# First mixture of experts of a four-layer decoder: the shared expert ahead of the routing, TensorE in written order, biases joined

## The chip, the cores and the metric

The kernel runs on one core of a Trainium2 chip, in one launch. The metric is device time in microseconds, from the program's start to its end; the time given is the median of three runs. One more execution was recorded by the hardware profiler, instruction by instruction; all durations come from that one. A core has five engines with an instruction queue each, which run in parallel and wait for each other on semaphores: TensorE (PE, with its weight loads shown as PEld), VectorE (DVE), ScalarE (ACT), GpSimd (POOL) and SyncE (SP, which here only issues DMAs).

## What is computed

The whole kernel is a decoder of four layers on x of 16 sequences x 128 tokens x 256 features in float32. Each layer adds a self-attention, a cross-attention and a feed-forward block to x, each behind a layer norm. The change concerns only the feed-forward block of layer 0, a mixture of 32 routed experts and one shared expert. Cut to this block, with x the 2048 normalized tokens:

```python
logits = x @ Wr + br                                   # 256 -> 32
aff = sigmoid(logits)
top_v, top_i = top_k(aff, 8)
top_w = top_v / (sum(top_v) + 1e-9)
w_full = zeros(T, 32); w_full[token, top_i] = top_w    # 8 of 32 are not zero
shared = (silu(x @ Wg_s + bg_s) * (x @ Wu_s + bu_s)) @ Wd_s + bd_s
gate = silu(einsum('th,ehi->eti', x, Wg) + bg)         # 256 -> 128 for each expert
up = einsum('th,ehi->eti', x, Wu) + bu
down = einsum('eti,eih->eth', gate * up, Wd) + bd      # 128 -> 256
return shared + einsum('te,eth->th', w_full, down)
```

Every expert is computed for every token; the weight w_full is zero where a token doesn't use it. The bias of the second product, bd, is weighted with w_full too, so that all 32 of them are one product: w_full @ bd.

## The kernel before

x stays in SBUF in four tiles `x[g]` (`NG` = 4 groups of `GB` = 4 sequences, so `GT` = 512 tokens a group, tokens on the 128 partitions). Tiles come from pools. `b1` is a pool of four PSUM banks of 512 float32 columns, `b2` one of two tiles of 1024 columns (two banks each). A tile asked for while all buffers of its tag are in use waits until an old one has been read out. Expert weights share seven SBUF slots (`slot`, 3 x 256 columns each) with other weights.

A scheduler orders the instructions of each engine: it may take an instruction ahead of an earlier one when it counts it ready sooner. Only what goes through `keep_in_program_order` (helpers `pinned` and `pinned_transpose`, L253 to L258) stays in the written order among itself. Before the change the feed-forward block uses `self.mm` (L162 to L168), which isn't pinned; the attention blocks ahead of it use pinned products.

`l0_ffn` (L563) has three parts.

1. For each group (L590 to L616): `layernorm` (statistics on VectorE at L201 and L202, square root on ScalarE and reciprocal on VectorE at L191 and L192, then normalization by VectorE's `tensor_scalar` at L205 into `h`); `hidden_T` (eight transposes by TensorE at L183 into two banks, which `evac` copies in turn by VectorE at L110 and ScalarE at L112 into `hT`); the router product of 8 matmuls with 32 columns; bias, sigmoid, and a chain of small VectorE instructions (the eight largest, sum, reciprocal, L603 to L611) which leaves the weights in `w_all`.
2. For each group (L618 to L628): four transposes of `w_all` at L622 into `wT`, a copy out, and for each sequence a bias product of two matmuls: `wT` with `bd` (32 rows, L166) and a row of ones with `bd_s` (1 row, L168). VectorE adds each result to x (L220).
3. For the shared expert (e = -1) and then the 32 experts, for each group, one unit (L629 to L649): `gate` and `up`, two matmuls of 512 columns each; SiLU with bias on ScalarE (L638) and a multiplication on VectorE (L639) into `gs`; `down`, four matmuls of 256 columns into a `b2` tile; and on VectorE the addition to x (L644 for the shared expert, L649 with the token's weight otherwise). 33 x 4 = 132 units.

A float32 matmul shows in the profile as two records: 132 x 2 matmuls of `gate` are 528 records. A transpose is one record.

Ahead of this block stands the cross-attention of layer 0. Its last work for group 3 is three additions by GpSimd (L548 to L550), which complete `x[3]`. Behind it stands the self-attention of layer 1; its preparation (`c2b`, `c2col` products on TensorE, centers and scales on VectorE) doesn't depend on x, and the scheduler places it inside the last experts. All DMAs of the block are issued by SP; those of the router weights, of `bd` and `bd_s` and of the first experts stand near the start of the program.

Of the kernel before, what the change touches and what calls it, by code (L numbers as in the profile page):

```python
# [8 lines left out]
F = mybir.dt.float32  # L9
BF = mybir.dt.bfloat16  # L10
U32 = mybir.dt.uint32
AF = mybir.ActivationFunctionType
ALU = mybir.AluOpType
# [3 lines left out]
P = 128  # L17
B = 16
T = B * P
DM = 256  # L20
DC = 192
NG = 4
GB = B // NG
GT = GB * P
# [5 lines left out]
class Decoder:  # L30
# [532 lines left out]
    def l0_ffn(self):  # L563
        nc = self.nc
        E, K = 32, 8
        wr = self.wp.tile([P, 2, E], F, tag="wr", name="wr")
        self.load_into(wr, "L0_ffn_Wr")
        bd = self.wp.tile([E, DM], F, tag="bd", name="bd")
        nc.sync.dma_start(out=bd, in_=self.a["L0_ffn_bd"])
        bds = self.row("L0_ffn_bd_s")  # L570

        def expert(e):
            w = self.slot([P, 3, DM], "expert")
# [7 lines left out]
            return w  # L581

        with self.tc.tile_pool(name="l0f", bufs=1) as wk:
            hTs = []

            w_all = wk.tile([P, B * E + P], F, tag="w_all", name="w_all")
            nc.gpsimd.memset(w_all[:, B * E :], 0.0)
            for g in range(NG):
                hT = self.hidden_T(self.layernorm(g))
                hTs.append(hT)  # L590
                ps = self.b1("router")[:, 0 : GB * E]
                for t in range(GB):
                    self.mm(ps[:, t * E : (t + 1) * E], [(hT[:, k, t * P : (t + 1) * P], wr[:, k, :]) for k in range(2)])
                aff = wk.tile([P, GB, E], F, tag="aff", name="aff", bufs=2)
                nc.vector.tensor_tensor(
                    aff, ps.rearrange("p (t e) -> p t e", e=E), self.b("L0_br").unsqueeze(1).to_broadcast([P, GB, E]), ALU.add
# [18 lines left out]
                    ALU.mult,  # L615
                )  # L616

            for g in range(NG):  # L618
                ps = self.b1("wT")
                for t in range(GB):  # L620
                    o = (g * GB + t) * E
                    nc.tensor.transpose(ps[:, t * P : (t + 1) * P], w_all[:, o : o + P], self.ident)  # L622
                wT = wk.tile([E, GT], F, tag="wT", name="wT", bufs=2)
                self.evac(wT, ps[0:E, :])
                for t in range(GB):
                    po = self.b1("bd")[:, 0:DM]
                    self.mm(po, [(wT[:, t * P : (t + 1) * P], bd)], bds)
                    self.add_x(g, t, po)  # L628
            for e in range(-1, E):  # L629
                w = expert(e)  # L630
                bg = self.c("L0_bg_s") if e < 0 else self.c("L0_bg")[:, e : e + 1]
                bu = self.c("L0_bu_s") if e < 0 else self.c("L0_bu")[:, e : e + 1]
                for g in range(NG):
                    pg, pu = self.b1("gate"), self.b1("up")
                    for i, ps in ((0, pg), (1, pu)):
                        self.mm(ps, [(w[:, i, k * P : (k + 1) * P], hTs[g][:, k, :]) for k in range(2)])
                    gs = wk.tile([P, GT], F, tag="gs", name="gs", bufs=3)
                    nc.scalar.activation(gs, pg, AF.Silu, bias=bg)  # L638
                    nc.vector.scalar_tensor_tensor(gs, pu, bu, gs, ALU.add, ALU.mult)  # L639
                    pd = self.b2("down").rearrange("p (t d) -> p t d", t=GB)  # L640
                    for t in range(GB):
                        self.mm(pd[:, t, :], [(gs[:, t * P : (t + 1) * P], w[:, 2, :])])
                    if e < 0:
                        nc.vector.tensor_tensor(self.x[g], self.x[g], pd, ALU.add)  # L644
                        continue
                    for t in range(GB):
                        o = (g * GB + t) * E + e
                        xt = self.x[g][:, t, :]
                        nc.vector.scalar_tensor_tensor(xt, pd[:, t, :], w_all[:, o : o + 1], xt, ALU.mult, ALU.add)  # L649

# [1571 lines left out]
```

## Time and profile before

| | before |
|---|---|
| median of three runs | 3755.2 us (3746.98 to 3758.4) |
| profiled execution | 3759.38 us, span 3757.7 us |
| TensorE (matmul) busy | 3406.1 us, 91% of the span |
| VectorE busy | 2112.9 us, 56% |
| ScalarE busy | 1414.6 us, 38% |
| GpSimd busy | 534.0 us, 14% |
| mean granted TensorE clock | 0.936 |
| first `gate`, start of last expert `down` in the trace | 436.8 us, 1123.2 us |

Times in the trace count from the span's start. A line of groups names the source line, the engine, the operation, the tiles written and read, the count, the busy time, the mean of one, and the idle time of the engine just before with what ended it. The chain that ended last is followed back from the last instruction, at each step to what released it. The list of waits gives for pairs of instructions how long the first one's engine sat idle until the second one ended. The clock column is the share of full TensorE clock that was granted. A busy TensorE isn't TensorE at full speed: at half clock it is as busy and takes twice as long.

### The profile page before, as it was taken

The page shows a single profiled execution, that of the slowest core. Times are in us where ns is not written, and L with a number is a line of the kernel's source. Part 1 is how long each engine was busy: PE and PEld are TensorE (multiplying, and loading weights), DVE is VectorE, ACT ScalarE, POOL GpSimd, SP SyncE. Part 2 cuts the span into 40 slices and gives each one's busy share as a digit, 9 for nine tenths or more (in the row PEclk, how much of TensorE's full clock was granted, in tenths as well). Part 3 has the DMA queues.
Part 4 walks back from the last instruction along what each step waited for, and adds up shares of the span by engine and source line. Part 5 has one row for each costly group of instructions (what it writes and reads, how often), then busy time and mean ns, then how long its engine had stood idle before and what let it go on. Part 6 is the DMA issues. An engine that isn't in the chain of part 4 may idle for free.

```text
span 3757.7 us, 51557 instructions
## 1 busy us (share of the span) xinstructions
PE 3406.1 (91%) x21008; PEld 1839.0 (49%) x21008; DVE 2112.9 (56%) x4132; ACT 1414.6 (38%) x1923; POOL 534.0 (14%) x686
## 2 busy tenths in 40 slices
PE   7987999999998899986799999467899999999999
PEld 4555655555556556663355566344222222224665
DVE  5545344444464444455577744514699999983440
ACT  2344111111124422226556523012477677774221
POOL 5423000000002321115100021012200000002100
PEclk9988699999998999998899999588799999999989
DMA  3000000000010100010000000083502020000000
GB/s 95 8 2 5 5 17 21 17 21 20 27 48 6 37 1 1 1 41 6 13 1 1 12 3 1 33 298 101 111 22 30 11 31 11 11 1 25 1 8 17
DMA packets 90485, 105.47 MB, mean 28 GB/s; under 512 B 11364, under 2 KB 72678, under 8 KB 89990
## 3 DMA queue, kind: packets, MB, share of 16 engines
q1 hardware_dynamic: 79672, 89.71, 9.0%
q0 software_dynamic: 4224, 6.43, 0.5%
q10 hardware_dynamic: 6352, 6.03, 0.5%
q8 instruction: 165, 2.70, 0.3%
q14 instruction: 72, 0.59, 0.1%
HBM read 85.53 MB, written 16.60 MB: 27 GB/s over the span
## 4 chain that ended last, share of the span: by engine, by line
PE 79%; DVE 9%; ACT 4%; POOL 3%; issue 3%; DMA 1%; POOLq 0%; ACTq 0%; DVEq 0%
PE acc L1784 7%; PE down L166 6%; PE gate L166 6%; PE up L166 6%; PE st L1784 6%; PE proj L255 6%; PE one L1784 4%; PE st L255 4%; PE qT L166 3%; PE o L255 2%; PE h L255 2%; PE rb L255 2%; PE v L886 2%; PE fc L166 2%; PE pr L166 2%
## 5 line engine op out<-in xcount | busy, mean ns | idle before, releaser
L1916 DVE TENSOR_REDUCE mx<-one 128x1 f32<-128x512 f32 x1024 | 660.1, 686 | 50.8 <-PE one L1784 40.5
L2039 ACT ACTIVATE e<-st 128x1024 f32<-128x1024 f32 x512 | 496.8, 1021 | 208.0 <-PE st L1784 206.9
L649 DVE SCALAR_TENSOR_TENSOR x<-down,w_all,x 128x256 f32<-128x256 f32 x512 | 212.2, 477 | 315.1 <-PE down L166 315.1
L638 ACT ACTIVATE gs<-gate,cols 128x512 f32<-128x512 f32 x132 | 90.7, 687 | 584.3 <-PE gate L166 584.3
L1784 PE MATMUL acc<-e,v 128*32 128x512 f32 x2048 | 288.9, 616 | 1.7 <-ACT e L2039 1.7
L1784 PE MATMUL st<-qp,kp 113*128 113x512 bf16 x1024 | 274.0, 388 | 9.8 <-ACT e L2039 5.7
L166 PE MATMUL gate<-hT,expert 128*128 128x512 f32 x528 | 250.0, 596 | 0.0
L166 PE MATMUL down<-expert,gs 128*128 128x256 f32 x1056 | 249.4, 379 | 0.5 <-DVE gs L639 0.5
L166 PE MATMUL up<-hT,expert 128*128 128x512 f32 x528 | 249.3, 594 | 0.0
L166 PEld LDWEIGHTS down<-expert,gs 128*128 128x128 f32 x1056 | 200.6, 190 | 84.0 <-DVE gs L639 31.7
L1784 PE MATMUL one<-kp,qp 16*128 16x512 bf16 x1024 | 224.1, 394 | 13.3 <-DVE mx L1916 7.3
L1784 PEld LDWEIGHTS <-qp 16*128 16x128 bf16 x1024 | 49.5, 91 | 332.1 <-issue 328.7
L166 PEld LDWEIGHTS gate<-hT,expert 128*128 128x128 f32 x528 | 100.7, 191 | 126.8 <-issue 126.5
L1784 PEld LDWEIGHTS <-kp 113*128 113x128 bf16 x1024 | 79.2, 98 | 148.8 <-issue 86.8
L988 DVE TENSOR_TENSOR cT<-o,rb 128x512 f32<-128x512 f32 x64 | 44.3, 691 | 164.2 <-ACT rb L986 164.2
L166 PEld LDWEIGHTS up<-hT,expert 128*128 128x128 f32 x528 | 100.9, 191 | 72.3 <-issue 65.7
L986 ACT COPY rb<-rb 128x512 f32<-128x512 f32 x64 | 37.5, 585 | 252.5 <-PE rb L255 252.5
L166 PE MATMUL qT<-hT,L_xattn_Wq 128*128 128x512 f32 x256 | 116.8, 610 | 8.6 <-DVE hT L110 4.5
L1187 DVE SCALAR_TENSOR_TENSOR xs<-xBC,cols,xs 128x508 f32<-128x508 f32 x144 | 106.1, 741 | 22.2 <-ACT xs L1183 18.8
L718 POOL MEMSET v<- 128x256 f32 x16 | 5.2, 329 | 794.6 <-DVE x L649 750.6
L255 PE MATMUL o<-e,v 128*32 128x128 f32 (+1 forms) x2048 | 105.8, 280 | 11.8 <-DVE nm L292 11.8
L639 DVE SCALAR_TENSOR_TENSOR gs<-up,cols,gs 128x512 f32<-128x512 f32 x132 | 99.0, 751 | 24.9 <-PE up L166 8.7
(511 smaller groups left out, 5697.7 us busy)
## 6 DMA issues: line engine op xcount, KB each, us to landing
W<-in_L_ffn_W_dram SPq DMA_DIRECT2D x46, 512.0 KB, 4.5
expert<-in_L_ffn_Wg_dram SPq DMA_DIRECT2D x32, 128.0 KB, 2.2
expert<-in_L_ffn_Wu_dram SPq DMA_DIRECT2D x32, 128.0 KB, 2.4
expert<-in_L_ffn_Wd_dram SPq DMA_DIRECT2D x32, 128.0 KB, 2.5
parts<-parts SPq DMA_DIRECT2D x16, 256.0 KB, 4.7
qp<-parts SPq DMA_DIRECT2D x28, 128.0 KB, 4.3
kp<-parts SPq DMA_DIRECT2D x12, 256.0 KB, 10.3
hs<-zero SPq DMA_DIRECT2D x23, 128.0 KB, 1.9
```

Of the source, the lines that this page charges most:

```text
L166: self.nc.tensor.matmul(out, lhsT, rhs, start=i == 0, stop=i == n - 1 and bias is None)
L255: self.tc.keep_in_program_order(self.nc.tensor.matmul(*a, **k))
L638: nc.scalar.activation(gs, pg, AF.Silu, bias=bg)
L639: nc.vector.scalar_tensor_tensor(gs, pu, bu, gs, ALU.add, ALU.mult)
L649: nc.vector.scalar_tensor_tensor(xt, pd[:, t, :], w_all[:, o : o + 1], xt, ALU.mult, ALU.add)
L886: nc.tensor.matmul(ps, l, r, start=True, stop=False)
L986: nc.scalar.copy(rb, ps)
L988: nc.vector.tensor_tensor(cT, po, rb, ALU.mult)
L1187: stt = lambda *a: pin(nc.vector.scalar_tensor_tensor(*a))
L1784: self.tc.keep_in_program_order(nc.tensor.matmul(*a, **k))
L1916: nc.vector.tensor_reduce(mx[:, t, kc, i : i + 1], pair[i], AX.X, ALU.max)
L2039: nc.scalar.activation(e[:, 2 * p : 2 * p + 2, :], ps, AF.Exp, scale=1.0 / 16.0)
```

## The change

- The bias rows are joined: `bd` has 33 rows, the last of them `bd_s`, and `wT` gets a row of ones (GpSimd memset), so that one matmul with 33 rows takes the place of two. The result of a group goes to one `b2` tile and is added to `x[g]` in one instruction.
- `layernorm` and `hidden_T` are written out as `tokens(g)`: the normalization is done by ScalarE (Identity with scale `rs` and bias `nm` = -mean x rs, a new small VectorE instruction), and both copies of the transposes by ScalarE.
- The shared expert comes first. `tokens(0)` and `tokens(1)` stand ahead of the loop; `router(g)` and `tokens(g + 2)` follow the g-th unit of the shared expert; `biases(g)` is spread over the units of expert 1.
- A unit is cut into `first` (gate, up, SiLU, multiplication) and `second` (down, addition to x), and `second` of a unit is written behind `first` of the next.
- All TensorE instructions of the block are pinned.

```diff
--- before.py
+++ after.py
@@ -565,9 +565,10 @@
         E, K = 32, 8
         wr = self.wp.tile([P, 2, E], F, tag="wr", name="wr")
         self.load_into(wr, "L0_ffn_Wr")
-        bd = self.wp.tile([E, DM], F, tag="bd", name="bd")
-        nc.sync.dma_start(out=bd, in_=self.a["L0_ffn_bd"])
-        bds = self.row("L0_ffn_bd_s")
+        bd = self.wp.tile([E + 1, DM], F, tag="bd", name="bd")
+        nc.sync.dma_start(out=bd[0:E, :], in_=self.a["L0_ffn_bd"])
+        nc.sync.dma_start(out=bd[E : E + 1, :], in_=self.a["L0_ffn_bd_s"])
         def expert(e):
             w = self.slot([P, 3, DM], "expert")
@@ -581,16 +582,41 @@
             return w
         with self.tc.tile_pool(name="l0f", bufs=1) as wk:
-            hTs = []
             w_all = wk.tile([P, B * E + P], F, tag="w_all", name="w_all")
             nc.gpsimd.memset(w_all[:, B * E :], 0.0)
-            for g in range(NG):
-                hT = self.hidden_T(self.layernorm(g))
+            hTs = []
+            def tokens(g):
+                st = self.small([P, GB, 6], "bnst")
+                mv = self.small([P, GB, 2], "bnmv")
+                rs = self.small([P, GB], "rstd")
+                nm = self.small([P, GB], "nmean")
+                for t in range(GB):
+                    nc.vector.bn_stats(st[:, t, :], self.x[g][:, t, :])
+                    nc.vector.bn_aggr(mv[:, t, :], st[:, t, :])
+                self.rsqrt(rs, mv[:, :, 1])
+                nc.vector.scalar_tensor_tensor(nm, mv[:, :, 0], -1.0, rs, ALU.mult, ALU.mult)
+                h = self.hp.tile([P, GB, DM], F, tag="h", name="h", bufs=2)
+                for t in range(GB):
+                    nc.scalar.activation(
+                        h[:, t, :], self.x[g][:, t, :], AF.Identity, scale=rs[:, t : t + 1], bias=nm[:, t : t + 1]
+                    )
+                hT = self.hp.tile([P, 2, GT], F, tag="hT", name="hT", bufs=5)
+                for k in range(2):
+                    ps = self.b1("tr")
+                    for t in range(GB):
+                        self.pinned_transpose(ps[:, t * P : (t + 1) * P], h[:, t, k * P : (k + 1) * P])
+                    nc.scalar.copy(hT[:, k, :], ps)
                 hTs.append(hT)
+            def router(g):
                 ps = self.b1("router")[:, 0 : GB * E]
                 for t in range(GB):
-                    self.mm(ps[:, t * E : (t + 1) * E], [(hT[:, k, t * P : (t + 1) * P], wr[:, k, :]) for k in range(2)])
+                    for k in range(2):
+                        self.pinned(
+                            ps[:, t * E : (t + 1) * E], hTs[g][:, k, t * P : (t + 1) * P], wr[:, k, :], start=k == 0, stop=k == 1
+                        )
                 aff = wk.tile([P, GB, E], F, tag="aff", name="aff", bufs=2)
                 nc.vector.tensor_tensor(
                     aff, ps.rearrange("p (t e) -> p t e", e=E), self.b("L0_br").unsqueeze(1).to_broadcast([P, GB, E]), ALU.add
@@ -615,38 +641,74 @@
                     ALU.mult,
                 )
-            for g in range(NG):
+            def biases(g):
                 ps = self.b1("wT")
                 for t in range(GB):
                     o = (g * GB + t) * E
-                    nc.tensor.transpose(ps[:, t * P : (t + 1) * P], w_all[:, o : o + P], self.ident)
-                wT = wk.tile([E, GT], F, tag="wT", name="wT", bufs=2)
-                self.evac(wT, ps[0:E, :])
+                    self.pinned_transpose(ps[:, t * P : (t + 1) * P], w_all[:, o : o + P])
+                wT = wk.tile([E + 1, GT], F, tag="wT", name="wT", bufs=2)
+                nc.gpsimd.memset(wT[E : E + 1, :], 1.0)
+                nc.scalar.copy(wT[0:E, :], ps[0:E, :])
+                yield
+                pd = self.b2("bd").rearrange("p (t d) -> p t d", t=GB)
                 for t in range(GB):
-                    po = self.b1("bd")[:, 0:DM]
-                    self.mm(po, [(wT[:, t * P : (t + 1) * P], bd)], bds)
-                    self.add_x(g, t, po)
-            for e in range(-1, E):
-                w = expert(e)
+                    self.pinned(pd[:, t, :], wT[:, t * P : (t + 1) * P], bd, start=True, stop=True)
+                nc.vector.tensor_tensor(self.x[g], self.x[g], pd, ALU.add)
+                yield
+            ws = {}
+            def first(e, g):
+                if g == 0:
+                    ws[e] = expert(e)
+                w = ws[e]
                 bg = self.c("L0_bg_s") if e < 0 else self.c("L0_bg")[:, e : e + 1]
                 bu = self.c("L0_bu_s") if e < 0 else self.c("L0_bu")[:, e : e + 1]
+                pg, pu = self.b1("gate"), self.b1("up")
+                for i, ps in ((0, pg), (1, pu)):
+                    for k in range(2):
+                        self.pinned(ps, w[:, i, k * P : (k + 1) * P], hTs[g][:, k, :], start=k == 0, stop=k == 1)
+                gs = wk.tile([P, GT], F, tag="gs", name="gs", bufs=3)
+                nc.scalar.activation(gs, pg, AF.Silu, bias=bg)
+                nc.vector.scalar_tensor_tensor(gs, pu, bu, gs, ALU.add, ALU.mult)
+                return e, g, gs
+            def second(e, g, gs):
+                pd = self.b2("down").rearrange("p (t d) -> p t d", t=GB)
+                for t in range(GB):
+                    self.pinned(pd[:, t, :], gs[:, t * P : (t + 1) * P], ws[e][:, 2, :], start=True, stop=True)
+                if e < 0:
+                    nc.vector.tensor_tensor(self.x[g], self.x[g], pd, ALU.add)
+                    return
+                for t in range(GB):
+                    o = (g * GB + t) * E + e
+                    xt = self.x[g][:, t, :]
+                    nc.vector.scalar_tensor_tensor(xt, pd[:, t, :], w_all[:, o : o + 1], xt, ALU.mult, ALU.add)
+            last, bias = None, None
+            tokens(0)
+            tokens(1)
+            for e in range(-1, E):
                 for g in range(NG):
-                    pg, pu = self.b1("gate"), self.b1("up")
-                    for i, ps in ((0, pg), (1, pu)):
-                        self.mm(ps, [(w[:, i, k * P : (k + 1) * P], hTs[g][:, k, :]) for k in range(2)])
-                    gs = wk.tile([P, GT], F, tag="gs", name="gs", bufs=3)
-                    nc.scalar.activation(gs, pg, AF.Silu, bias=bg)
-                    nc.vector.scalar_tensor_tensor(gs, pu, bu, gs, ALU.add, ALU.mult)
-                    pd = self.b2("down").rearrange("p (t d) -> p t d", t=GB)
-                    for t in range(GB):
-                        self.mm(pd[:, t, :], [(gs[:, t * P : (t + 1) * P], w[:, 2, :])])
+                    now = first(e, g)
+                    if last:
+                        second(*last)
+                    last = now
                     if e < 0:
-                        nc.vector.tensor_tensor(self.x[g], self.x[g], pd, ALU.add)
-                        continue
-                    for t in range(GB):
-                        o = (g * GB + t) * E + e
-                        xt = self.x[g][:, t, :]
-                        nc.vector.scalar_tensor_tensor(xt, pd[:, t, :], w_all[:, o : o + 1], xt, ALU.mult, ALU.add)
+                        router(g)
+                        if g + 2 < NG:
+                            tokens(g + 2)
+                    if bias:
+                        next(bias)
+                        bias = None
+                    if e == 1:
+                        bias = biases(g)
+                        next(bias)
+            second(*last)
```

## The prediction

> **What bounds the kernel now.** I began with the page's chain that ended last: 79% of it is TensorE, so the question is what TensorE does in this block, and when. The sum by stage (start and end, length, then busy time and instruction count of TensorE, its weight loads, VectorE, ScalarE, GpSimd, then granted clock, DMA share, GB/s) splits the block in two:
>
> ```profile
> 366.00:436.00 70.00, 53.86 (x175) 42.88 (x176) 33.84 (x129) 10.26 (x17) 7.25 (x4) 0.50 0.01 4
> 436.00:465.00 29.00, 29.00 (x78) 15.62 (x77) 9.06 (x10) 3.44 (x5) 0.00 (x0) 0.88 0.04 12
> 550.00:650.00 100.00, 100.00 (x310) 58.65 (x309) 47.49 (x100) 13.05 (x19) 0.00 (x0) 1.00 0.06 18
> ```
>
> The expert loop has TensorE busy for 100 of 100 us at full clock. One unit (one expert, one group of four sequences) lasts 5.157 us: 8 records of 512 columns at 0.429 us and 8 of 256 at 0.216. 132 units are 680.7 us, and only removed products could shorten them. The 70 us ahead of it run at half clock. The critical chain there (start, length, what):
>
> ```profile
> 367.50 7.20 DVE h L205 x3
> 384.04 6.25 PE router L166 x30
> 402.85 1.22 PE bd L166 x2
> 404.07 0.85 PE bd L168 x2
> 436.90 3.71 PE gate L166 x4
> 440.61 2.85 PE up L166 x4
> 443.46 1.72 PE gate L166 x4
> 445.17 1.73 PE down L166 x8
> ```
>
> Router, transposes and bias products are serial work ahead of the first gate at 436.90. A pair of bias records costs 0.85 us (0.427 each), against 0.216 for the same 256 columns of `down` in the loop. The gate products start cold (3.71 us for 4 records) and reach 1.72 after 6.6 us. The timeline shows why the stage starts late, and how the block ends:
>
> ```profile
> 367.37 2.34 POOL L548 TENSOR_TENSOR qp<-qp,bcast 128x1024 f32<-128x1024 f32 x1 [7.00 <-DVE rstd L192]
> 367.42 8.24 DVE L205 TENSOR_SCALAR h<-x,bnmv,rstd 128x256 f32<-128x256 f32 x6
> 372.33 0.48 PE L183 MATMUL tr<-ident,h 128*128 128x128 f32 x1 [1.94 <-DVE h L205]
> ...
> 1119.99 1.88 PE L166 MATMUL c2b<-c,ones 128*128 128x512 f32 x4
> 1121.71 1.89 PE L166 MATMUL down<-expert,gs 128*128 128x256 f32 x8
> ```
>
> Six normalizations take 8.24 us because three of them crawl, one per GpSimd addition (367.37, 369.78, 372.20, last end 374.54). At the end the scheduler slid `c2b`, a product of the next layer, ahead of the last `down`, so 1123.43 - 1.72 = 1121.7 is the comparable end. The list of waits in the loop (470 to 1125; total, times, longest):
>
> ```profile
> PEld down L166 <- DVE gs L639: 30.5, 123, 1.3
> PE down L166 <- DVE gs L639: 0.5, 1, 0.5
> ```
>
> The weight load waits for `gs` 0.25 us a time, but the products behind it lose 0.5 us in all: the loop is already pipelined.
>
> [...]0.50 after the idle gap that ends at 369.91, full speed some 5 to 6.6 us into the gate products. [...]here the clock stayed 0.50 from 411 to 436.9 although TensorE was busy 24 of 26 us with 32-row and 1-row bias products and a few transposes. [...]
>
> **The change, part by part.**
>
> *Start of the first gate.* The statistics and the first reciprocals stay where they are (done by 367.5). The three new `nmean` instructions have two SBUF inputs and come just as GpSimd starts. A free one would be ready at 368.0; a blocked one gets one gap per addition, as `h` did: 369.9, 372.3, 374.7. I take blocked. Then ScalarE normalizes: the nearest rows, 128x256 with a per-partition operand, are 505 ns (L1178) and 489 ns (L745), so 0.50 each. Group 0: 369.9 to 371.9. Group 1, with the two `hT` copies of group 0 (0.585 each) in its queue: 372.35 + 4 x 0.50 + 2 x 0.585 = 375.5. Its last transpose of half 0 and the four of half 1 at 0.21 (cold): 376.65. In the written order `gate` of the shared expert stands right there, and its weights landed near 25 us. First gate 376.7 instead of 436.9: **60.2 us earlier**; free `nmean` would make it 374.5.
>
> *Work that moves into the loop*, at full clock, where TensorE has no slack, so all of it counts. Transposes and router records are 0.208 us cold (6.25 / 30), 0.107 taken for warm: 16 transposes (groups 2, 3) 1.7, 64 router records 6.8, 16 transposes of the weights 1.7. Joined biases: 16 matmuls, 32 records of 256 columns at 0.2155, 6.9. **Together 17.1 us.** Removed outright: 32 one-row records, 13.7 us cold. The two DMAs for `bd` are as many as before, at the same place of SP's queue (24 us); the four new memsets run on an idle GpSimd.
>
> *ScalarE in the shared expert.* Sigmoid, SiLU and square root now alternate: ten table loads of 1.28 us fall there, against four before, with 8 copies, 8 normalizations, 4 SiLU. [...]the row here is 1283 ns. I walked the four units with the written order of each queue. TensorE waits 0.4 us (for `gs` of unit 0 ahead of gate 1); the closest other place is gate 2, which waits for a bank that VectorE drains behind the x addition, 0.35 us in hand; group 3's `h` is 1.9 us early. [...] Behind a late ScalarE stands `gs`, then `down` and every later bank.
>
> *Steady loop.* gate, up, previous down is the same cycle of records. `gs` is needed 5.2 us after its `up` ends, not 1.7, and is ready about 1.0 after (0.2 + 0.75): slack 4.1 for 0.75. VectorE's queue holds 0.75 + 4 x 0.415 = 2.4 of 5.16 us, in four units 1.2 more for the bias addition. Pinning therefore costs nothing; without this slack it would, once per unit. Expert weights land in 2.5 us and are needed again after some 100 us of seven slots; SP's order is unchanged.
>
> *End.* The last `down` waits for `gs` behind the previous `down` (1.72 against 1.0), so no gap; `c2b` and `c2col` follow in place of half of them preceding. Behind the first group of the next layer each queue is unchanged in order, so what is gained here is carried to the end.
>
> **Sum.** 60.2 - 17.1 - 0.4 = 42.7. The cold start of the gates (6.56 us for 8 records where 3.43 is warm) is paid once in both. I leave 1 us for some sixteen new waits whose latency no row shows: **41.7 us**. Against the profiled execution, 3759.4 with span 3757.7, that is 3717.7 and span 3716; the median, 3755.2, lies 4.2 lower, and gives **3713.5 us**. The median is what I forecast. Less than 0.3% of it, 11.3 us, can't be told from no change.
>
> **Rivals.**
>
> A, the above, chance 0.70: 3713.5, its own range 3705 to 3722 (free `nmean` -2.2, no waits -1[...], an idle gap or two +4).
>
> B, the clock stays low, 0.14. Router and transposes put 2.5 us of weak work between dense units, and weak work did not warm TensorE in 25 us before. Against it: in the attention ahead (353 to 363) transposes and 32-column products with small gaps kept 0.93. Cold to about 410 adds 14 us, cold for the whole shared expert and a unit or two beyond 27: 3727 to 3740.
>
> C, ScalarE becomes the bound of the shared expert, 0.06. If each of four units waited 2.5 us for its table loads, +10: 3723. For it: ten loads are 12.8 us of some 30. Against: TensorE's written order puts 2.5 us of router and transposes where ScalarE catches up.
>
> D, slower, 0.05. Place: the written order of TensorE in the loop. Where the scheduler had pulled `gate` ahead of `down` by readiness, a pinned `down` or `gate` that finds `gs` or its bank not ready holds everything behind it, 132 times. From 0.32 us per unit (41.7 / 132) it decides; at 0.5 us the time is 3755 - 42 + 66 = 3779. The slack of 4.1 us speaks against it. A clock that stays low to 465 would also just reach zero.
>
> E, more gained, 0.03: warm early, gate at 374.5 and a quicker start of the next layer, 3702.
> That the order isn't taken over can be left out: the changed program has `gate` right behind the first 16 transposes. The remaining 0.02 is a loss in the next layer's first group, where the order of VectorE differs, about even.
>
> Range: A with the near half of B and C, 3703 to 3733. Faster by over 0.3% is A, B, C and E less a little, 0.92; same 0.03; slower 0.05.
>
> **What would show it.** Right: first gate at 375 to 378, the last expert `down` at 1077 to 1081 (before 1123.4), no bias or router record ahead of the gate, granted clock near 1.00 from 383, unit 5.16 us. `nmean` in steps of 2.4 us shows the blocked case. Wrong: a clock of 0.50 past 390 (B), TensorE idle for ScalarE's `hT` or `gs` between 380 and 410 (C), a unit over 5.3 us (D), or the last `down` 42 us earlier but the end not, which would be a later stage that I have not read.

## The result and the profile after

| | before | after |
|---|---|---|
| median | 3756.8 us (four runs, 3746.98 to 3759.03) | 3716.43 us (four runs, 3713.4 to 3721.63) |
| ratio after / before, 95% interval | | 0.990 (0.9884 to 0.9916) |
| profiled execution | 3759.38 us, span 3757.7 us | 3721.63 us, span 3719.9 us |
| mean granted TensorE clock | 0.936 | 0.941 |
| first `gate` in the trace | 436.83 us | 374.82 us |
| kT, the first dense product of the next layer | 1126.56 us | 1086.15 us |

The changed kernel is 40.4 us faster by medians; 3713.5 us was predicted, with 3703 to 3733 as the range. The profiled execution is the slowest of the four.

The sum by stage of the changed kernel (columns as in the prediction):

```profile
366.00:376.00 10.00, 6.22 (x18) 3.84 (x19) 4.26 (x14) 7.13 (x14) 8.23 (x6) 0.50 0.01 2
376.00:380.00 4.00, 4.00 (x6) 1.55 (x6) 0.00 (x0) 2.61 (x5) 0.00 (x0) 0.56 0.00 0
380.00:386.00 6.00, 6.00 (x33) 4.13 (x32) 3.38 (x22) 5.91 (x9) 0.00 (x0) 1.00 0.00 0
436.00:465.00 29.00, 29.00 (x104) 17.54 (x103) 13.77 (x23) 4.47 (x7) 1.03 (x2) 1.00 0.05 14
465.00:1010.00 545.00, 545.00 (x1693) 321.34 (x1692) 258.92 (x529) 75.82 (x108) 0.00 (x0) 1.00 0.07 21
1010.00:1020.00 10.00, 7.82 (x19) 4.51 (x18) 8.58 (x12) 1.10 (x2) 0.00 (x0) 0.83 0.00 1
```

The half-clock stretch, 70 us before, is down to some 14. From 380 on the clock is full, and TensorE is busy all the time but for one place near 1012. The timeline of the start:

```profile
366.00 2.34 POOL L548 TENSOR_TENSOR qp<-qp,bcast 128x1024 f32<-128x1024 f32 x1 [7.10 <-DVE rstd L192]
366.05 2.45 DVE L599 SCALAR_TENSOR_TENSOR nmean<-bnmv,rstd 128x4 f32<-128x4 f32 x3
368.45 2.57 ACT L602 ACTIVATE h<-x,nmean,rstd 128x256 f32<-128x256 f32 x5 [3.60 <-DVE nmean L599]
```

All three `nmean` instructions are done within 2.45 us: the first lasts 2305 ns (366.05 to 368.36), as long as GpSimd's addition (366.00 to 368.34), the next two 150 and 149 ns. The first is blocked, and the others slip through the gap behind it: they begin at 368.28 and 368.35, the next addition at 368.42. The critical chain through the shared expert (start, length, what):

```profile
375.02 3.41 PE gate L255 x4
378.44 2.33 PE up L255 x4
380.77 1.71 PE router L255 x16
382.48 0.91 PE tr L258 x8
383.38 1.72 PE gate L255 x4
```

Router and transposes stand between dense units, back to back, at full clock: 2.6 us a unit for the first two units. And the groups of the page (operation, tiles, count, busy time and mean ns, idle time before with what ended it):

```profile
L255 PE MATMUL down<-expert,gs 128*128 128x256 f32 x1056 | 250.9, 381 | 2.2 <-DVE gs L675 2.2
L255 PE MATMUL gate<-hT,expert 128*128 128x512 f32 x528 | 250.3, 597 | 0.0
```

No `gate` waits for anything; all 132 `down` together wait 2.2 us. That is a single wait, which the timeline shows:

```profile
1006.98 6.55 DVE L743 RECIPROCAL log_scales<-log_scales 128x1024 f32<-128x1024 f32 x1
1013.45 0.65 DVE L675 SCALAR_TENSOR_TENSOR gs<-up,cols,gs 128x512 f32<-128x512 f32 x1
1014.15 3.54 PE L255 MATMUL down<-expert,gs 128*128 128x256 f32 x8 [2.18 <-DVE gs L675]
1017.49 2.06 PE L255 MATMUL gate<-hT,expert 128*128 128x512 f32 x4
...
1086.15 5.36 PE L166 MATMUL kT<-hT,L_attn_W_q 128*128 128x512 f32 x8 [0.35 <-DVE hT L110]
1091.35 3.60 PE L166 MATMUL qT<-hT,L_attn_W_q 128*128 128x512 f32 x8
```

The next layer's reciprocal, 6.55 us, stands ahead of `gs` in VectorE's queue; TensorE is idle for 2.18 us, and the `down` after it runs at half clock (next start 3.34 us later, where 1.72 is usual). kT starts at half clock too (5.20 us to the start of qT; 3.54 before).

### The profile page after: what moved, and what is told of

It reads as the page before. It is cut to its first block, busy times and chain, and to the rows that moved or that the text cites. A ratio compares the mean times of both kernels' runs of the same rounds, so it can differ in the third digit from the quotient of the medians.

```text
span 3719.9 us, 51499 instructions
## 1 busy us (share of the span) xinstructions
PE 3379.5 (91%) x20976; PEld 1816.7 (49%) x20976; DVE 2095.8 (56%) x4102; ACT 1433.7 (39%) x1951; POOL 537.3 (14%) x690
## 4 chain that ended last, share of the span: by engine, by line
PE 80%; DVE 9%; ACT 4%; POOL 3%; issue 3%; DMA 1%; SPq 0%; POOLq 0%; ACTq 0%; DVEq 0%
PE acc L1846 7%; PE down L255 6%; PE gate L255 6%; PE up L255 6%; PE st L1846 6%; PE proj L255 6%; PE one L1846 4%; PE st L255 4%; PE qT L166 3%; PE o L255 2%; PE h L255 2%; PE rb L255 2%; PE v L948 2%; PE pr L166 2%; PE kT L948 2%
## 5 line engine op out<-in xcount | busy, mean ns | idle before, releaser
L1249 DVE SCALAR_TENSOR_TENSOR xs<-xBC,cols,xs 128x508 f32<-128x508 f32 x144 | 106.1, 741 | 22.2 <-ACT xs L1245 18.8
L255 PE MATMUL o<-e,v 128*32 128x128 f32 (+1 forms) x2048 | 105.7, 280 | 11.8 <-DVE nm L292 11.8
```

Source lines behind the costliest of these rows:

```text
L255: self.tc.keep_in_program_order(self.nc.tensor.matmul(*a, **k))
L1249: stt = lambda *a: pin(nc.vector.scalar_tensor_tensor(*a))
```

## The experiments

**How they are compared.** One execution differs from the next by more than some of these edits cost. Over the 14 traces the last additions of GpSimd ahead of the block (L548, where nothing is changed yet) begin between 365.6 and 373.9 us, and the rest of the program from the first `yk` on (a product of the next layer) takes 2604 to 2619 us. So beside the medians I give the block's own length within a trace: from the start of those additions to the first `gate`, and to the start of kT. On that scale the two traces of the changed kernel differ by 0.2 us.

| kernel | to the first gate | to kT | median, us | ratio to before (95%) |
|---|---|---|---|---|
| before | 69.46 | 759.19 | 3754.6 to 3758.6 | |
| after | 8.82 | 720.15 | 3716.4 | 0.990 (0.988 to 0.992) |
| after, again | 8.81 | 720.34 | 3711.4 | 0.989 (0.987 to 0.991) |
| routing first | 51.02 | 743.19 | 3737.5 | 0.994 (0.992 to 0.996) |
| biases unjoined | 8.82 | 733.70 | 3735.5 | 0.994 (0.993 to 0.996) |
| unjoined, 128 rows | 8.83 | 724.44 | 3724.0 | 0.991 (0.989 to 0.993) |
| whole units | 8.81 | 883.37 | 3884.6 | 1.035 (1.033 to 1.036) |
| unpinned | 5.73 | 712.56 | 3710.0 | 0.988 (0.986 to 0.989) |
| unpinned, again | 5.73 | 712.31 | 3711.2 | 0.987 (0.985 to 0.990) |
| before with 128-row biases | 53.32 | 740.13 | 3744.4 | 0.997 (0.995 to 0.998) |
| normalization on VectorE | 10.69 | 718.22 | 3714.8 | 0.989 (0.987 to 0.992) |
| reciprocal in four | 8.81 | 716.01 | 3708.8 | 0.987 (0.984 to 0.989) |
| the same, warmed up | 9.62 | 714.48 | 3712.2 | 0.988 (0.985 to 0.990) |
| the same, second tokens later | 6.05 | 716.59 | 3717.4 | 0.990 (0.988 to 0.992) |

My theory, as predicted: the gain is the serial half-clock stretch ahead of the first gate, whose work moves to where TensorE is dense and at full clock. The rivals: the joined biases, the written order, or the change of engine make it.

**1. The routing ahead of the shared expert again.**

```diff
-            tokens(0)
-            tokens(1)
+            for g in range(NG):
+                tokens(g)
+                router(g)
+            for g in range(NG):
+                for _ in biases(g):
+                    pass
...
-                    if e < 0:
-                        router(g)
-                        if g + 2 < NG:
-                            tokens(g + 2)
```

(The two places that spread the biases over expert 1 go too.)

> The changed kernel's pieces, joined biases and written order, but the tokens and routers of all four groups and all bias products stand ahead of the shared expert again. My theory (the gain is the stretch ahead of the first gate, which runs in sequence at half clock, moved to where TensorE runs at full clock): nearly all of the gain goes. The first gate comes at 415 to 432 us instead of 374.8 and the last down of the layer some 30 to 45 us later than in the changed kernel, the time 3745 to 3762 us. What is left against the kernel before is at most the joined biases (32 records fewer, 7 us at full clock, 14 us at half clock). Rival (the joined biases and the written order make the gain, not the place of the routing): the time stays within 10 us of the changed kernel's 3716 us.

The gate comes at 421.4 us in the trace, within what I expected, but 51.0 us after the additions, 18.4 fewer than before the change; and the time, 3737.5 us, is clearly below my 3745 to 3762. About half of the gain stays (18.3 of 40.4 us by the medians; 16.0 of 39.0 by the block's length). I had written off what the other parts do in that stretch. From the additions to the first bias product it is 30.6 us instead of 35.5 (ScalarE normalizes and copies, and the order differs; which of these makes the 4.9 us isn't shown), and the bias stage is 20.4 us instead of 34.0:

```profile
417.73 3.75 PE L255 MATMUL bd<-bd,wT 33*128 33x256 f32 x8 [0.79 <-issue]
421.41 3.66 PE L255 MATMUL gate<-hT,expert 128*128 128x512 f32 x4
```

The joined records still run at half clock (0.46 us each: 3.68 from start to end of the eight), but they are half as many. So the place is worth 23.0 us of the 39.0 and the other parts 16.0: neither theory holds alone. The prediction's sum has both (13.7 us for the removed one-row records at half clock, 60.2 for the gate in all), but I didn't carry it into this expectation.

**2. Two bias products again, in the new places.**

```diff
-                    self.pinned(pd[:, t, :], wT[:, t * P : (t + 1) * P], bd, start=True, stop=True)
+                    self.pinned(pd[:, t, :], wT[:, t * P : (t + 1) * P], bd, start=True, stop=False)
+                    self.pinned(pd[:, t, :], self.ones[0:1, 0:P], bds, start=False, stop=True)
```

> The changed kernel with the two biases added by two products again, in the same places in expert 1. 32 one-row records more, at full clock in the loop: at 0.22 to 0.24 us each, as the joined ones take, 6.9 to 7.7 us, so 3723 to 3724 us, and units of expert 1 of 9.4 to 9.6 us instead of 7.67. A rival (one-row products hide behind the other work once they are in the loop): no difference, units of 7.7 us.

Not 7 us but 13.6 in the block, and 19 to 24 by the medians. The timeline of expert 1 shows the rest:

```profile
443.80 0.59 PE L255 MATMUL bd<-bd,wT 32*128 32x256 f32 x2
444.23 0.59 PE L255 MATMUL bd<-L_ffn_bd_s,ones 1*128 1x256 f32 x2
444.75 0.66 PE L258 MATMUL wT<-ident,w_all 128*128 128x128 f32 x4
445.25 3.26 PE L255 MATMUL gate<-hT,expert 128*128 128x512 f32 x4
448.29 2.25 PE L255 MATMUL up<-hT,expert 128*128 128x512 f32 x4
```

The records themselves cost what I expected, but behind each stretch of 3.7 to 5.3 us of bias products and transposes the `gate` starts at half clock: 3.0 to 3.5 us to the next start instead of 1.72, four times of four. TensorE is never idle there. The units take 9.4, 11.5, 11.8 and 11.1 us. In the changed kernel the same stretch is 2.4 us of joined products and transposes, and no gate behind it is slow. The sum by stage (first column of busy time TensorE, clock third from the end) shows when the clock changes:

```profile
445.62:449.02 3.40, 3.40 (x5) 1.35 (x4) 0.46 (x1) 0.88 (x2) 0.00 (x0) 0.50 0.00 0
449.03:455.85 6.82, 6.82 (x28) 4.77 (x26) 2.41 (x5) 0.20 (x1) 0.00 (x0) 1.00 0.00 0
455.86:459.26 3.40, 3.40 (x8) 1.92 (x8) 1.22 (x1) 0.57 (x1) 0.00 (x0) 0.50 0.00 0
```

It falls at 445.61, rises at 449.02, falls at 455.85 and rises at 459.26: distances of 3.41, 6.83 and 3.41 us. In all 14 traces, with 1062 records of the clock (72 in that of the kernel before, 78 in the first of the changed kernel), it is 0.50 or 1.00, and two changes that follow each other lie a multiple of 3.41 us apart (to 0.01 us).

**3. Why the clock falls: rows or stretch.** Two kernels widen the bias products by zeros to 128 rows, with as many records of as many columns in the same places: the kernel before, and the one just shown.

```diff
-        bd = self.wp.tile([E, DM], F, tag="bd", name="bd")
-        nc.sync.dma_start(out=bd, in_=self.a["L0_ffn_bd"])
-        bds = self.row("L0_ffn_bd_s")
+        bd = self.wp.tile([P, DM], F, tag="bd", name="bd")
+        nc.gpsimd.memset(bd, 0.0)
+        nc.sync.dma_start(out=bd[0:E, :], in_=self.a["L0_ffn_bd"])
+        bds = self.wp.tile([P, DM], F, tag="bds", name="bds")
+        nc.gpsimd.memset(bds, 0.0)
+        nc.sync.dma_start(out=bds[0:1, :], in_=self.a["L0_ffn_bd_s"])
```

(`wT` gets all 128 rows, and the one-row weights become the full tile of ones.)

> The kernel before, with its bias products widened from 32 and 1 rows to 128 rows by zeros (as many records, as many columns, the same places). It asks why TensorE stood at half clock there although it was busy. If the number of rows decides whether the clock rises: it reaches 1.00 some 4 to 10 us into the bias stage, the stage of 34 us shrinks by 10 to 16 us, the first gates run at full clock, and the time is 10 to 18 us below the kernel before, 3739 to 3747 us. If rows do not matter (the clock follows time, or the number of records): no difference, 3756 us within 4.

The bias stage, from the first bias product to the first `gate`, of the kernel before and of this one:

```profile
402.85:436.83 33.98, 31.83 (x76) 22.72 (x77) 8.89 (x34) 2.43 (x3) 0.00 (x0) 0.50 0.00 0
```

```profile
401.37:421.82 20.45, 18.26 (x76) 15.11 (x77) 8.92 (x34) 2.46 (x3) 0.00 (x0) 0.89 0.00 1
```

As many matmuls, no busier (89% of the stage instead of 94%), at a mean clock of 0.89 instead of 0.50. The bias records reach full speed 4.4 us after the first of them and keep it; the stage takes 20.45 us instead of 33.98, and the first gates start at full speed (3.44 us for gate and up instead of 6.46). The stage ahead, which the edit leaves alone, is 2.6 us shorter in this trace: its router products ran at full clock for 3.4 us from 385.4 on, which they didn't in the kernel before. In all the block is 19.1 us shorter. The median of eight runs, 3744.4, is only 10.2 below that of before. It lies in the range that I gave, but whether the other runs warm up as this trace did isn't shown.

> The changed kernel with the two biases in two products again, as in the unjoined run, but each widened to 128 rows by zeros: as many records and columns as there, in the same places. In the unjoined run each stretch of 3.9 us of bias products was followed by gates at half clock (3.1 to 3.6 us instead of 1.72). If the few rows are the cause: the gates behind stay at 1.8 us, units of expert 1 take 9.4 to 9.7 us instead of 10.9 to 12.8, and the time is 3722 to 3726 us instead of 3735. If the stretch of bias products itself is the cause, whatever its rows: the gates at half clock stay, with 3735 us.

```profile
445.09 0.59 PE L255 MATMUL bd<-bd,wT 128*128 128x256 f32 x2
445.52 0.59 PE L255 MATMUL bd<-bds,ones 128*128 128x256 f32 x2
445.95 0.60 PE L258 MATMUL wT<-ident,w_all 128*128 128x128 f32 x4
446.39 1.88 PE L255 MATMUL gate<-hT,expert 128*128 128x512 f32 x4
```

The same stretch, with as many records and TensorE as busy, with 128 rows: no slow gate. Units take 9.06, 9.05, 9.05 and 8.62 us (I had expected 9.4 to 9.7), and the block is 9.3 us shorter than with 32 and 1 rows. So the few rows of these records, not their number, let the clock fall here. Joining the biases was worth 13.6 us in the loop: 4.3 with full rows (the records cost some 5.6 us, while the first gates happened to be 1.2 us less cold in that trace), and 9.3 because the clock didn't fall behind the shorter stretch.

**4. First and second products of a unit together.**

```diff
-                    now = first(e, g)
-                    if last:
-                        second(*last)
-                    last = now
+                    second(*first(e, g))
```

> The changed kernel with each unit's second products written directly behind its first ones, in the pinned order. My theory: pinning needs the split. Each down then waits for its own gs, which comes 1.0 to 1.25 us after the up ends (SiLU, product and semaphores), in each of the 132 units: 130 to 165 us longer, 3846 to 3881 us, and units of 6.2 to 6.4 us instead of 5.16. Rival (the split makes no difference, the gain would come with any order): within 5 us of the changed kernel.

```profile
L255 PE MATMUL down<-expert,gs 128*128 128x256 f32 x1056 | 266.4, 396 | 129.3 <-DVE gs L675 128.1
```

3884.6 us, a little above the range that I gave. Units of 6.34 us, 1.18 more than 5.16; over 132 units 156 us of the 163.2 by which the block is longer, most of the rest at the reciprocal. This is the price of a written order without slack, and the place where "slower" was to be had: the split pays for the pin.

**5. The same program, nothing pinned.**

```diff
-                        self.pinned(
+                        nc.tensor.matmul(
...
-                        self.pinned_transpose(ps[:, t * P : (t + 1) * P], h[:, t, k * P : (k + 1) * P])
+                        self.loose_transpose(ps[:, t * P : (t + 1) * P], h[:, t, k * P : (k + 1) * P])
```

(and likewise for the other five products and transposes of the block)

> The changed kernel with nothing of the layer written in a fixed order on TensorE; the program's order is the same, the scheduler puts the instructions. My theory: the written order itself gains nothing, because the steady loop was bound by TensorE in both. The time is within 4 us of the changed kernel, 3712 to 3720 us; the wait of 2.2 us of the down behind the next layer's reciprocal goes, since other gates and ups are taken meanwhile. Rival (the pin gains): over 10 us slower than the changed kernel, with waits of downs for gs in the loop.

> The unpinned kernel once more, since in its first trace the layer (from GpSimd's last additions ahead of it to kT of the next layer) took 712.6 us and in both traces of the changed kernel 720.2 and 720.3, while the times overlap (3704 to 3712 against 3709 to 3722 us). If leaving the order to the scheduler is really 7.6 us shorter in the layer (3.1 ahead of the first gate, some 4 at the reciprocal, where the down takes 3.5 us at half clock after its wait of 2.2): the layer again within 0.5 us of 712.6, the first gate 5.7 us after the additions, no wait of a down, and a median of 3706 to 3711 us. If the first was a lucky execution: a layer of 716 to 720 us and 3712 to 3717 us.

Twice the block is 7.6 to 8.0 us shorter than with the pin, beyond what I expected the first time. Two things make it. The scheduler puts half of the first gate ahead of the second group's last transposes (5.73 instead of 8.82 us after the additions; the first `up` is through 3.7 us earlier). And at the reciprocal it takes the next gate meanwhile:

```profile
1011.38 1.88 PE L675 MATMUL up<-hT,expert 128*128 128x512 f32 x4
1013.10 1.88 PE L675 MATMUL gate<-hT,expert 128*128 128x512 f32 x4
1014.81 1.02 PE L675 MATMUL up<-hT,expert 128*128 128x512 f32 x2
1015.67 1.89 PE L684 MATMUL down<-expert,gs 128*128 128x256 f32 x8
```

The reciprocal lasts 6.55 us there too; no `down` waits, which is worth 4.0 us. By time the ten runs (3701.5 to 3720.1, median 3710.4) and the nine of the changed kernel (3708.9 to 3721.6, median 3714.3) overlap: the block's length shows that the pin costs, the medians alone don't.

**6. The changed kernel again**, beside experiments 3 (the second kernel) and 9.

> The changed kernel itself, unaltered, beside the next two on one chip, so that versions a few us apart are compared on the same chip: 3716 us within 4. It also shows once more what varies between executions: whether kT of the next layer, after the 16 one-column products of c2col, starts at half clock (5.2 us, as in the first trace of the changed kernel) or at full clock (3.5 us, as in seven of the nine other traces), and whether the wait of 2.2 us for the reciprocal is there (it should be, each time).

3711.4 us, just below the range that I gave. The wait is there as expected (2.44 us, the `down` behind it at half clock again), and kT starts at full clock this time. (Eight, not seven, of the nine other traces had it so; over all 14 it is ten.)

**7. Normalization on VectorE.**

```diff
-                    nc.scalar.activation(
-                        h[:, t, :], self.x[g][:, t, :], AF.Identity, scale=rs[:, t : t + 1], bias=nm[:, t : t + 1]
+                    nc.vector.tensor_scalar(
+                        h[:, t, :], self.x[g][:, t, :], mv[:, t, 0:1], rs[:, t : t + 1], ALU.subtract, ALU.mult
```

> The changed kernel with the tokens' normalization on VectorE (subtract the mean, multiply by rstd) instead of on ScalarE. My theory: on VectorE the pieces of h stand against GpSimd's additions again. Ten pieces must go ahead of the first gates; if each is held for up to one addition of 2.4 us, as the first nmean of the changed kernel was (2.3 us), the first gate comes 3 to 15 us later than 374.8, with the time 3719 to 3731 us. Rival (the engine of the normalization does not matter): the gate within 1 us.

```profile
375.33 0.47 PE L258 MATMUL tr<-ident,h 128*128 128x128 f32 x1 [5.72 <-DVE h L600]
377.75 0.48 PE L258 MATMUL tr<-ident,h 128*128 128x128 f32 x1 [1.94 <-DVE h L600]
380.17 3.51 PE L258 MATMUL tr<-ident,h 128*128 128x128 f32 x14 [1.94 <-DVE h L600]
383.48 2.13 PE L255 MATMUL gate<-hT,expert 128*128 128x512 f32 x4
```

Only the first pieces wait, one for each addition; with the last addition over, the other nine come in a rush. The gate is 1.9 us later, below the least that I gave. And nothing is lost: behind fourteen transposes without a gap the gates run nearly at full clock (3.68 us for gate and up instead of 5.79). The block is 1.9 us shorter than in the changed kernel, about what the `down` behind the reciprocal, not slow in this trace, accounts for. So the engine of the normalization isn't what makes the gain here. (Both copies of the transposes stay on ScalarE; moving those back is untested.)

**8. The reciprocal cut in four, and the gates warmed up.**

```diff
-            nc.vector.reciprocal(obf, obf)
+            for i in range(4):
+                nc.vector.reciprocal(obf[:, 256 * i : 256 * i + 256], obf[:, 256 * i : 256 * i + 256])
```

> The changed kernel with the next layer's reciprocal of 128x1024 on VectorE cut into four of 128x256. My theory for the wait of 2.18 us at one down product near 1012 us: gs stands behind the 6.55 us reciprocal in VectorE's queue. Cut, gs waits for 1.64 us at most, which the unit's reserve covers: the wait goes to below 0.3 us and the last down of the layer comes 2 us earlier, 3714 us. Rival (something else holds gs): the wait stays at about 2.2 us.

```profile
1014.88 1.75 DVE L744 RECIPROCAL log_scales<-log_scales 128x256 f32<-128x256 f32 x1
1016.55 0.65 DVE L675 SCALAR_TENSOR_TENSOR gs<-up,cols,gs 128x512 f32<-128x512 f32 x1
1018.69 1.74 DVE L744 RECIPROCAL log_scales<-log_scales 128x256 f32<-128x256 f32 x1
```

`gs` goes between the pieces, and no `down` waits (3708.8 us by the median, for 3714 expected). From first gate to kT it is 707.2 us instead of 711.3: 4.1 us, twice the wait, because the half-clock `down` behind it goes as well.

The second kernel adds, ahead of and between the first transposes, products of the ones with the shared expert's weights, whose result isn't used:

```diff
+            def warm(n, cols):
+                ps = self.b2("warm")[:, 0:cols]
+                for _ in range(n):
+                    self.pinned(ps, self.ones, wide[:, 0:cols], start=True, stop=True)
...
+            warm(4, 512)
             tokens(0)
+            warm(1, 256)
             tokens(1)
```

> The changed kernel with the cut reciprocal of the run before and eleven extra full-size products of the ones with the shared expert's weights ahead of and between the first transposes, whose result is not used. They fill TensorE's wait for the tokens. If the first gates are slow because TensorE was idle before them: gate and up take 3.5 us together instead of 6.2, the extra work costs nothing on the path or at most 0.5 us, and the time is 2 to 2.7 us below the run with the cut reciprocal, 3711.5 us. If the clock does not react to such work within the few us there are: the same time as with the cut reciprocal.

```profile
380.41 1.88 PE L255 MATMUL gate<-hT,expert 128*128 128x512 f32 x4
```

The gates do run at full clock, 2.35 us faster, but start 0.8 later, more than I allowed, and the block gains 1.5 us against the cut reciprocal. The medians (3712.2 and 3708.8) can't resolve that.

**9. On top of that, the second group's tokens behind the first gate and up.**

```diff
-            tokens(0)
-            warm(1, 256)
-            tokens(1)
+            tokens(0)
...
                     if e < 0:
+                        if g == 0:
+                            tokens(1)
                         router(g)
```

> Cut reciprocal and warm-up products as in the run before with them, and the tokens of the second group behind the first gate and up instead of ahead of them. The first gate then needs one group's transposes: it should come 5.6 us after GpSimd's last additions begin, instead of 8.8 in the changed kernel and 9.6 in the run with the warm-up products; the second group's transposes fit in behind the up, at full clock, with nothing waiting. The start of the next layer, counted from the same additions, comes 3 to 4.5 us earlier than with the warm-up alone (711 us after them instead of 714.5, and 720.2 in the changed kernel): 3707 to 3709 us. If the gate is held by something else than the transposes of group 2, or the second gate then waits for its hT: no gain against the warm-up, 3712 us.

The first gate came nearly as expected, at 6.05 us, but the gain was given back at once, as the timelines of TensorE and ScalarE show:

```profile
380.32 1.87 PE L255 MATMUL router<-wr,hT 128*128 128x32 f32 x16
382.02 0.53 PE L258 MATMUL tr<-ident,h 128*128 128x128 f32 x3
384.06 1.33 PE L258 MATMUL tr<-ident,h 128*128 128x128 f32 x5 [1.51 <-ACT h L610]
385.18 3.62 PE L255 MATMUL gate<-hT,expert 128*128 128x512 f32 x4
...
381.91 1.28 ACT L634 ACT_TABLE_LOAD   x1
383.20 0.31 ACT L634 ACTIVATE aff<-aff 128x128 f32<-128x128 f32 x1
383.42 0.58 ACT L610 ACTIVATE h<-x,nmean,rstd 128x256 f32<-128x256 f32 x1
```

A piece of the third group's `h` stands behind the table load and sigmoid of the first router on ScalarE. TensorE waits 1.51 us, and the weak stretch before gate 1 (transposes, router, transposes, wait) grows to 5.7 us: gate and up start at half clock, 5.9 us instead of 3.44. The block is 2.1 us longer than with the warm-up alone, not 3 to 4.5 shorter, and the median is 3717.4 us, not 3707 to 3709. Here ScalarE is a bound, which it wasn't with the tokens in their place.

## Why the prediction was right, and where its steps were off

The time, 3716.4 for 3713.5 us predicted, and the mechanism hold. In the trace the block is 39.0 us shorter where the sum gave 41.7. That the sum is only 2.7 us off is in part luck: the steps below were wrong by 5.7 us one way and by 3.0 the other. Step by step:

- *Start of the first gate*, 60.2 us earlier predicted, 60.6 measured (69.46 to 8.82). Right in sum. "A blocked one gets one gap per addition" was wrong for the second and third `nmean`: only the first was held, and all went through in one gap. The first group's `h` started 2.45 us after the additions began, as in the blocked case, but the second group's followed without a further wait. So the gate, 8.82 us after the additions began, falls between my two values, 9.3 (blocked) and 7.1 (free). That an `nmean` can be held at all was my estimate from the steps of `h`; the 2305 ns of the first one show it.
- *Work that moves into the loop*, 17.1 us predicted, 18.8 measured. Router and transposes of the tokens: 8.8 for 8.5. The biases: 10.0 us (four times 7.67 - 5.16) for 8.6; eight joined records take 1.92 us instead of 1.72, four transposes 0.44 to 0.50 instead of 0.43, and the `down` ahead of the joined records 1.82 instead of 1.73. That term was a little undersized.
- *The joined biases* I priced by their records alone. Experiments 2 and 3 show that joining also kept the clock: 9.3 of the 13.6 us that it is worth in the loop.
- *ScalarE*, 0.4 us of waits predicted, none measured: `gate` has 0.0 idle. Rival C fell. The upper end of A's range, 3722, rested in part on slower table loads, which no trace showed: where ScalarE's queue was full, a load took 1.28 us and its function started 1.29 us after the load did (378.51 and 379.80 in the trace of the changed kernel). Experiment 9 shows how close it stood.
- *Cold start of the gates*, once in both: 6.46 us before, 5.79 after, so 0.7 gained, not even.
- *Steady loop, "pinning therefore costs nothing"*: the step that failed. In the loop it is right (5.16 us a unit, TensorE busy 545 of 545 us, `gs` off the path), and experiment 4 shows that the slack is what makes it right. But I counted only the block's own work in VectorE's queue. The next layer's reciprocal, 6.55 us, is longer than the slack of 4.1 by 2.4, and the pinned `down` waited 2.2 us; it and the `gate` behind it then ran 1.8 us slow. That is rival D's mechanism, once instead of 132 times. Ahead of the first gate the pin costs another 3.1 us (experiment 5). I hadn't seen that the scheduler could start the gate before all transposes were through.
- *The clock* rose by 380 us and stayed, through router and transposes of 2.6 us a time: rival B fell. What would have made it true is now known: stretches of 3.7 us and more with 32 and 1 rows lost the clock (experiment 2). The prediction had no measure of how long a weak stretch may last, so that its own, of 2.4 to 2.6 us, stayed short enough is luck. Its "kept 0.93" for 353 to 363 was misread too: the clock was 1.00 there, and 0.93 is the mean up to 366.
- *End*: kT started 4.83 us after the last `down` had run, 1.72 of them `c2b`, which stood ahead of it before; without `c2b` it is 3.1 us in both. The last `down` ended at 1081.3, just behind the 1077 to 1081 that I had named. That kT started at half clock (1.7 us) is not the change's doing: a second trace of the same kernel doesn't show it, and one with the order of before does (experiment 3, first kernel).

The measured terms give 60.6 - 18.8 - 4.0 (wait and slow `down`) + 0.7 (cold start) + 0.5 (the kernel before waited 0.47 us at its reciprocal) = 39.0 us, the block's difference. The 1 us that I left for new waits, and the 0.4 for ScalarE, are not seen.

No version is shown to beat the changed kernel by its median. Leaving the same program to the scheduler has the shortest block (712.3 and 712.6 us against 720.2 and 720.3).

## What to carry to other kernels

Serial work of weak products ahead of a dense loop cost twice here: its own time and half clock (70 us at 0.50). Move it between dense units in short pieces (2.4 to 2.6 us kept the clock here, 3.7 us with few rows lost it), and join products of few rows, since a TensorE that was busy with them all the time still lost the clock (1.00 to 0.50 in experiment 2). A written order was free here only while its slack (4.1 us) exceeded the longest single instruction in the queue that it waited for, that of the next stage included (6.55 us); look for that instruction before pinning. Time a stage by two events inside the trace when whole executions scatter by more than the edit.

## What the runs showed of the hardware that I had not expected

- Rows mattered to the clock: the same bias records with 128 rows instead of 32 and 1 brought it to 1.00 within 4.4 us where it had stayed at 0.50 for 34 us, and kept gates at 1.72 us that took 3.0 to 3.5 otherwise. They weren't everything: 30 router records in a row, 128 rows but 32 columns, ran at 0.50 for 6.45 us in the kernel before. And transposes came ahead of full clock: in experiment 7 fourteen without a gap filled 2.9 of the 3.4 us behind which it rose.
- The clock fell without any idle time: stretches of 3.7 us and more with 32 and 1 rows lost it four times of four, those of 2.4 us with 33 rows never. Its changes lay multiples of 3.41 us apart (experiment 2), and not at the same place of the program in every trace.
- That explains most of what varied between these executions. At the reciprocal the `down` was slow in four of six traces with the pin, the split and a wait of 2.2 to 2.5 us. In these four, 2.2 us or more of the wait lie between two neighbouring points of the 3.41 us grid; in the two others a point cuts it (0.69 and 1.49 us, 0.32 and 1.85 us). With the waits of experiment 4, idle time of 1.92 us or more in one such stretch cost the clock, of 1.85 or less didn't (there the `down` behind a wait of 1.92 us took 3.34 us to the next start, the one behind 2.15 us, cut by a point, 1.83); so it didn't take a stretch that was idle throughout. Ahead of kT stand 1.7 us of one-column products, transposes and a gap, 3.1 us in all; kT was slow in 4 of 14 traces, those where 3.0 to 3.1 us of this fell into one stretch (one other, with 3.0, wasn't slow).
- A wait on GpSimd's additions was not paid by every instruction. One small `nmean` waited (2305 ns) and the two behind it passed in the same gap (150 and 149 ns); of the 128x256 normalizations of experiment 7 one passed in each gap, so that of twelve, 10.75 us in all, the first three waited.
